# Masks of the ranked layer on GpSimd, written as complements, and their exponents split evenly between VectorE and ScalarE

## The chip, the cores and the metric

One core of one Trainium2 chip runs the whole program. The metric is the device time of an execution in microseconds (us), from runs repeated three times; lower is better. A profiled execution of the same kernel gives the trace from which all durations below are read. The engines are TensorE (PE, with its weight loads shown as PEld), VectorE (DVE), ScalarE (ACT), GpSimd (POOL) and SyncE (SP), which here only issues transfers.

## The reference

A graph of N = 3327 nodes with 64 features each passes through four layers, every one of the form x = x + layer(relu(layernorm(x))) with the same dense adjacency matrix `adj` (3327 x 3327 floats, few of them non-zero):

- layer 0: two gated cells; each multiplies `adj` by the features and feeds a GRU
- layer 1, "ranked": only the last 100 neighbours of a row count, and each weighs half of the one after it
- layer 2: three products with `adj * adj` (element by element), each followed by a linear map
- layer 3: two products with `adj`, each followed by a linear map and tanh

So `adj` is read for eight products, called steps k = 0 to 7 in the kernel. Step 2 is the ranked one:

```python
mask = (adj != 0).astype(support.dtype)
rank = jnp.cumsum(mask, axis=1)
deg = rank[:, -1:]
k = jnp.minimum(deg, float(MAX_NEIGH))
pos = rank - (deg - k)
w = mask * jnp.where(pos > 0, DECAY ** (k - pos), 0.0)
out = w @ support + bias
```

The weight of a neighbour is a power of two that depends only on how many neighbours come after it in its row.

## The kernel before, in words

The nodes are padded to 26 blocks of 128 (two halves of 13 blocks). The adjacency matrix lies transposed in memory, so a tile is 128 source nodes (tile number q, 26 of them) by the target nodes of one group. There are two groups of target columns, `GROUPS`: group 0 holds chunks 0 and 1 (3 + 3 blocks of 128), group 1 holds chunks 2 and 3 (3 + 4 blocks). Each group is taken from both halves of the nodes, so a tile has two halves (s = 0, 1) of 768 columns in group 0 and of 896 in group 1. `Tile.load` (L405) issues one transfer per tile on SP's queue into one of 20 slots (`slots`, shown as `adj` in the profile); the slot must have been given up by its last user, `Tile.used`.

The steps are interleaved in pairs per group so that one load serves two steps: `joint(0, 1)` is steps 1 and 2 of group 0, `joint(1, 2)` is steps 2 and 3 of group 1. The function `run` walks a fixed list of units (step, chunk, tile), and looks ahead: up to 44 units for loads, 24 for masks, 3 for the expansion. All engines work through their instructions in the order in which this walk emits them; nothing is reordered at run time. Side work of each chunk (GRU, layer norm and so on, `after_0` to `after_7`) is a generator that is advanced by an amount of PE time (`spend`).

For the ranked step a tile goes through these stages:

1. `make_mask` (L466) writes the mask, 1.0 where `adj` is not zero, as bfloat16 for 127 of the 128 rows, in two "pieces" (one per half). Between the two, L471 has POOL issue a small transfer that puts the counts of all later blocks (`totals`) into row 127 of the mask. After the second piece the raw tile has been `used` once, which, in group 0 at step 2, gives its slot up. Masks lie in slots too, two to a slot; `Mask` takes one and `free` returns it after the tile's last expansion.
2. `expand` (L510 to L523) multiplies the mask by a triangular matrix `tri` on PE (L307). `tri` has 2^14 on its diagonal and -2^7 below it, and row 127 takes the counts with -2^7, so each sum is the bit pattern of the weight's exponent, short of the constant `BITS`. Adding `BITS` and clamping at zero, written as a 16-bit integer and read as bfloat16, is the weight. This last operation is L521 on DVE (a constant added, then the maximum with zero) or L523 on ACT (Relu with `bitsb` as bias). A rule with several cases picks DVE or ACT for half s = 1; half s = 0 is always on ACT.
3. `propagate` (L607) multiplies the weights by the features, held as three bfloat16 terms (`both`), which `in_three` splits off.

POOL also does one operation of each layer norm (L845, a power of -1/2), issues the transfers that collect the last row of each block (`lasty`, L928), and clears the scratch of `last_sources` (L564), whose two small transfers (L568) stand in SP's queue among the loads. The counts come from an earlier pass (`count`, L542) over masks of all 128 rows, which L466 also writes, on DVE; there are 104 pieces of this kind and 104 of the ranked kind.

Of the kernel before, what the change touches and what calls it, by code (L numbers as in the profile page):

```python
# [9 lines left out]
F32 = mybir.dt.float32  # L10
BF16 = mybir.dt.bfloat16
I16 = mybir.dt.int16
AF = mybir.ActivationFunctionType
ALU = mybir.AluOpType
# [30 lines left out]
N, D = 3327, 64  # L45
P = 128
NB = 13
# [8 lines left out]
GROUPS = [(0, 1), (2, 3)]  # L56
GWM = 7 * P
EPS = 1e-5
TWO7 = float(2 ** 7)
TWO27 = float(2 ** 27)  # L60
CAP = 100.0
BITS = (CAP - 128.0) * TWO7
# [8 lines left out]
PLAIN, RANKED, SQUARED = range(3)  # L71
# [12 lines left out]
def chunk_of(b):  # L84
    return next(c for c, (b0, b1) in enumerate(CH[:NC]) if b0 <= b < b1)
# [6 lines left out]
def upper(n):  # L92
    return slice(n * D, (n + 1) * D)
# [3 lines left out]
def kernel(  # L97
# [9 lines left out]
    nc = tc.nc  # L107

    const = ctx.enter_context(tc.tile_pool(name="const", bufs=1))
# [8 lines left out]
    for g0, g1 in (CH[0], (CH[0][1], NB)):  # L118
# [15 lines left out]
    make_identity(nc, ident)  # L134
    tri = const.tile([P, P], BF16, name="tri")
    behind = const.tile([P, NQ - 1 + D], BF16, name="behind")
    bitsb = const.tile([P, 1], F32, name="bitsb")
    totals = [const.tile([P, sum(CH[c][1] - CH[c][0] for c in g) * P], BF16, name=f"totals{i}")
              for i, g in enumerate(GROUPS)]
    lastw = [const.tile([P, sum(CH[c][1] - CH[c][0] for c in g) * P], I16, name=f"lastw{i}")  # L140
             for i, g in enumerate(GROUPS)]
# [7 lines left out]
                            compare_op=ALU.is_gt, fill=0.0, base=2 - P, channel_multiplier=1)  # L149

    def load_cell(cell):
        nc.sync.dma_start(out=stage[upper(0), :7 * D].rearrange("p (w f) -> p w f", f=D),
                          in_=weights[:, (W1, W2)[cell]:(W1, W2)[cell] + 7])
        if cell == 0:
            nc.sync.dma_start(out=stage[upper(0), 7 * D:], in_=bias_cols)
# [82 lines left out]
    def more_constants():  # L238
        nc.gpsimd.memset(stage, 0.0)
        nc.gpsimd.memset(cells, 0.0)  # L240
        for c in range(NC):
            for h in range(2):
                nc.gpsimd.memset(both[c][upper(h), h], 0.0)
        nc.gpsimd.memset(bd, 0.0)
        yield 5.0
        load_cell(0)
        yield 20.0
        unfold_cell(0)
        yield 1.0

        full = work.tile([P, P], BF16, name="t2")
        nc.gpsimd.memset(full, -TWO7)
        nc.gpsimd.affine_select(out=tri, in_=full, pattern=[[-1, P]], compare_op=ALU.is_gt, fill=0.0,
                                base=0, channel_multiplier=1)
        nc.gpsimd.affine_select(out=tri, in_=tri, pattern=[[-1, P]], compare_op=ALU.not_equal, fill=TWO7 * TWO7,
                                base=0, channel_multiplier=1)
        nc.gpsimd.memset(tri[:, P - 1:P], 0.0)
        nc.gpsimd.memset(bitsb, BITS)
        nc.gpsimd.memset(lasty, 0.0)
        wide = work.tile([P, P], F32, name="t2")  # L260
        nc.gpsimd.memset(wide, 0.0)

        for i, (bi, bh) in enumerate(((BI1, BH1), (BI2, BH2))):
            nc.vector.tensor_add(bsum[:, i], bcol[:, bi:bi + 2], bcol[:, bh:bh + 2])

        nc.vector.tensor_scalar(wide[0:D], wide[0:D], bcol[0:D, BL1:BL1 + 1], None, op0=ALU.add)
        yield 3.0
        i, ps = take()
        mm(ps[:, :D], wide, ident[:, :D])
        nc.vector.tensor_copy(brow[:, 3], ps[:, :D])  # L270
        give(i)
        yield 1.0
        yield from fold_cell(0)
        for c in range(NC):
            yield 1.0
            ahead_of_cell(c)
        yield 50.0
        load_cell(1)
        yield 20.0
        unfold_cell(1)  # L280
        yield from fold_cell(1)
        yield 30.0
        for h in range(2):
            nc.sync.dma_start(out=bd[upper(h), :, upper(h)], in_=weights[:, WL1:WL3])
            for i in range(2):
                nc.sync.dma_start(out=w3[upper(h), :, i], in_=weights[:, WL3 + (h + i) % 2:NW:2])
        yield 5.0
        nc.sync.dma_start(
            out=brow[:, 0:3],
            in_=bass.AP(tensor=bias_rows.tensor, offset=bias_rows.offset, ap=[[0, P], [D, 3], [1, D]]),  # L290
        )
        yield 22.0
        yield from fold_hops()
# [5 lines left out]
    def width(c):  # L299
        return blocks(c) * P  # L300

    def mm(out, lhsT, rhs, start=True, stop=True):


        for h in range(2):
            hs = slice(h * D, (h + 1) * D)
            nc.tensor.matmul(out[hs], lhsT[:, hs], rhs, start=start, stop=stop)  # L307
# [21 lines left out]
    def give(i):  # L329
        released[i] = max(released) + 1  # L330
        (idle_sums if i < 4 else idle_temps).append(i)
# [34 lines left out]
    def finish(c):  # L366
        while c in tasks:
            advance(c)
# [16 lines left out]
    sums = {}  # L385
# [70 lines left out]
    pieces = deque()  # L456

    relief = {"squares": False, "pieces": False}

    def make_mask(t, kind):  # L460

        t.mask = Mask(t.w)
        rows = P - 1 if kind == RANKED else P

        def piece(half):
            nc.vector.tensor_scalar(t.mask.view[:rows, half], t.view()[:rows, half], 0.0, None, op0=ALU.not_equal)  # L466
            if half == 0 and kind == RANKED:

                for ch in GROUPS[t.g]:
                    finish(("count", ch))  # L470
                nc.gpsimd.dma_start(out=t.mask.view[P - 1:P], in_=totals[t.g][t.q:t.q + D + 1:D, :])  # L471
            if half == 1:
                t.used()

        pieces.extend([(t, 0, piece), (t, 1, piece)])
# [8 lines left out]
    def expand(k, c, t):  # L484

        if k == COUNT:
            return None
        w = width(c)
        if t is SPECIAL:
            g = c // 2  # L490
            w0 = (CH[c][0] - CH[GROUPS[g][0]][0]) * P
            finish(NC + 1 + g)
            return lastw[g][:, w0:w0 + w].bitcast(BF16)
        if KIND[k] == PLAIN or (KIND[k] == SQUARED and t.in_place):
            return t.view(c)
        if KIND[k] == SQUARED:
            room = Mask(t.w)
            wide = room.view.rearrange("p s w -> p (s w)").bitcast(F32)[:, :2 * w].rearrange("p (s w) -> p s w", s=2)
            square(wide, t.view(c), t.q + c)
            squared[k, c, t] = room  # L500
            return wide
        wide = work.tile([P, 2, CWM], I16, name="e", bufs=4)[:, :, :w]

        mask_pieces(t=t)
        for s in range(2):
            i, ps = take()
            mm(ps[:, :w], tri, t.mask.view[:, s, t.cols(c)])  # L510
            own = chunk_of(t.q % NB) in GROUPS[t.g]
            busy = any((k - 1, ch) in sums for ch in GROUPS[t.g])
            if t.g == 1 and not own and not relief["squares"]:

                on_vector = s and c == GROUPS[1][1]
            elif relief["pieces"]:
                on_vector = s and (t.q + c) % 4
            else:
                on_vector = s and (own if t.g == 0 and (own or busy) else c == GROUPS[t.g][1] or t.g == 1 and not own)
            if on_vector:  # L520
                nc.vector.tensor_scalar(wide[:, s], ps[:, :w], BITS, 0.0, op0=ALU.add, op1=ALU.max)  # L521
            else:
                nc.scalar.activation(wide[:, s], ps[:, :w], AF.Relu, bias=bitsb)  # L523
            give(i)
        spend(STREAM_US * w / CWM * 0.5)
        if c == GROUPS[t.g][1]:
            t.mask.free()
        return wide.bitcast(BF16)
# [29 lines left out]
    def last_sources(g):  # L558

        w = sum(width(c) for c in GROUPS[g])  # L560
        w0 = CH[GROUPS[g][0]][0] * P
        room = Mask(w)
        v = room.view.rearrange("p s w -> p (s w)").bitcast(F32)
        nc.gpsimd.memset(v, 0.0)  # L564
        yield 4.0
        rows = adjT.rearrange("(q p) (s n) -> q p s n", p=P, s=2)
        for s in range(2):
            nc.sync.dma_start(out=v[s * D:s * D + NQ], in_=rows[:, P - 1, s, w0:w0 + w])  # L568
        yield 12.0
        nc.vector.tensor_scalar(v, v, 0.0, 129.0 * TWO7, op0=ALU.not_equal, op1=ALU.mult)  # L570
        for c in GROUPS[g]:
            finish(("count", c))
        yield 1.0
        nc.vector.scalar_tensor_tensor(v, totals[g], -TWO7, v, op0=ALU.mult, op1=ALU.add)
        yield 1.5
        nc.scalar.activation(lastw[g], v, AF.Relu, bias=bitsb)
        room.free()

    def propagate(k, c, t, rhs, first, last):
# [506 lines left out]
```

## Time and profile before

| what | value |
|---|---|
| median of the runs | 706.3 us (705.96 to 706.94) |
| the profiled execution, first to last instruction (its span) | 703.7 us |
| PE, weight loads, DVE, ACT, POOL busy | 679.8, 372.9, 350.1, 271.8, 80.0 us |
| L466, all mask pieces, on DVE | 208 pieces, 114.0 us |
| of these the ranked ones: 127x768 and 127x896 | 52 at 567 ns and 52 at 619 ns |
| L521 on DVE | 63 in all |
| L523 on ACT | 145 in all |
| L471 on POOL | 52, mean 607 ns |
| SP's loads of tiles | 130 of 768 KB, 104 of 896 KB |

The profiled execution's own time is its span, which lies 2.6 us under the median of the runs; the difference is what surrounds the program, and is taken as constant. Times inside the trace count from the start of the span. Busy time is the sum of an engine's instructions, and the number after a group of instructions is the mean duration of one. "Idle before" a group names what released its engine. In the timeline a row can hold several instructions (the number after x).

### The profile page before, as it was taken

The page shows a single profiled execution, that of the slowest core. Times are in us where ns is not written, and L with a number is a line of the kernel's source. Part 1 is how long each engine was busy: PE and PEld are TensorE (multiplying, and loading weights), DVE is VectorE, ACT ScalarE, POOL GpSimd, SP SyncE. Part 2 cuts the span into 40 slices and gives each one's busy share as a digit, 9 for nine tenths or more (in the row PEclk, how much of TensorE's full clock was granted, in tenths as well). Part 3 has the DMA queues.
Part 4 walks back from the last instruction along what each step waited for, and adds up shares of the span by engine and source line. Part 5 has one row for each costly group of instructions (what it writes and reads, how often), then busy time and mean ns, then how long its engine had stood idle before and what let it go on. Part 6 is the DMA issues. An engine that isn't in the chain of part 4 may idle for free.

```text
span 703.7 us, 12628 instructions
## 1 busy us (share of the span) xinstructions
PE 679.8 (97%) x5100; PEld 372.9 (53%) x5100; DVE 350.1 (50%) x746; ACT 271.8 (39%) x422; POOL 80.0 (11%) x114
## 2 busy tenths in 40 slices
PE   1999999999999999999999999999999999999997
PEld 1454666643556787677444444333344444344586
DVE  7556835643997889847523105425271565005101
ACT  1014100122146888888998206832166600000101
POOL 4300000002284233111100000000000000000000
PEclk9999999999999999999999999999999999999999
DMA  9999996089686952683799649973998399927991
GB/s 344 401 385 404 406 405 241 2 314 398 209 279 253 371 177 76 246 297 96 265 390 343 245 151 409 405 276 100 398 366 271 107 391 406 406 81 276 402 403 45
DMA packets 68549, 201.31 MB, mean 286 GB/s; under 512 B 7228, under 2 KB 8228, under 8 KB 68492
## 3 DMA queue, kind: packets, MB, share of 16 engines
q1 hardware_dynamic: 65596, 199.46, 75.9%
q8 instruction: 40, 0.66, 0.4%
q10 hardware_dynamic: 720, 0.85, 0.3%
q0 software_dynamic: 2176, 0.20, 0.2%
q14 instruction: 17, 0.14, 0.1%
HBM read 199.45 MB, written 0.85 MB: 285 GB/s over the span
## 4 chain that ended last, share of the span: by engine, by line
PE 91%; DVE 7%; issue 0%; ACT 0%; DMA 0%; POOL 0%; ACTq 0%; DVEq 0%; POOLq 0%
PE sum L607 77%; PE temp L307 5%; PE temp L542 2%; PE temp L876 2%; PE sum L307 1%; DVE adj L466 1%; PE temp L774 1%; PE sum L876 1%; DVE e L521 1%; DVE st L842 1%; DVE adj L901 1%; DVE t L836 1%; DVE y L841 0%; DVE st L834 0%; DMA xs<-in_x 0%
## 5 line engine op out<-in xcount | busy, mean ns | idle before, releaser
L607 PE MATMUL sum<-adj,y 128*64 128x384 f32 (+3 forms) x3016 | 534.5, 502 | 0.7 <-DVE y L849 0.6
L607 PEld LDWEIGHTS sum<-adj,y 128*64 128x64 f32 x3016 | 243.5, 137 | 237.3 <-issue 212.4
L440 ACT ACTIVATE adj<-adj 128x768 f32<-128x768 f32 (+1 forms) x176 | 144.2, 893 | 45.8 <-PE sum L607 21.9
L466 DVE TENSOR_SCALAR adj<-adj 128x768 bf16<-128x768 f32 (+3 forms) x208 | 114.0, 597 | 39.8 <-PE temp L542 31.8
L824 ACT COPY both<-sum 64x384 f32<-64x384 f32 (+3 forms) x17 | 8.1, 478 | 192.6 <-PE sum L607 191.4
L607 PE MATMUL sum<-e,both 128*64 128x384 bf16 (+1 forms) x624 | 78.5, 339 | 0.5 <-DVE e L521 0.5
L523 ACT ACTIVATE e<-temp,bitsb 128x384 int16<-128x384 f32 (+1 forms) x117 | 66.0, 605 | 15.1 <-PE temp L307 9.9
L825 DVE COPY both<-sum 64x384 f32<-64x384 f32 (+3 forms) x17 | 9.6, 569 | 110.5 <-ACT both L824 110.5
L307 PE MATMUL temp<-adj,tri 128*64 128x384 bf16 (+1 forms) x332 | 56.8, 341 | 0.5 <-DVE e L521 0.2
L442 DVE TENSOR_TENSOR adj<-adj 128x768 f32<-128x768 f32 (+1 forms) x32 | 30.6, 1005 | 52.1 <-DMA adj<-in_adjT 33.4
L845 POOL TENSOR_TENSOR st<-st,mhalf 128x6 f32<-128x6 f32 (+1 forms) x16 | 24.0, 1498 | 283.2 <-DVE st L843 279.5
L607 PEld LDWEIGHTS <-both 128*64 128x64 bf16 x624 | 46.6, 110 | 15.5 <-issue 2.2
L307 PEld LDWEIGHTS <-tri 128*64 128x64 bf16 x416 | 33.5, 110 | 15.3 <-issue 7.1
L521 DVE TENSOR_SCALAR e<-temp 128x384 int16<-128x384 f32 (+1 forms) x49 | 30.1, 617 | 21.1 <-ACT e L523 10.5
L471 POOL DMA_DIRECT2D adj<-totals x52 | 31.5, 607 | 51.2 <-PE temp L307 40.9
L803 DVE STREAM_TRANSPOSE both<-y 32x96 f32<-32x96 f32 (+1 forms) x128 | 35.6, 278 | 2.9
L542 PE MATMUL temp<-adj,behind 128*64 128x384 bf16 x208 | 30.3, 339 | 0.9 <-DVE adj L466 0.7
L819 DVE STREAM_TRANSPOSE y<-t 32x96 f32<-32x96 f32 (+1 forms) x64 | 17.8, 278 | 24.9 <-ACT t L810 24.0
L542 PEld LDWEIGHTS <-behind 128*64 128x64 bf16 x208 | 17.0, 110 | 17.6 <-issue 15.9
L755 DVE COPY t<-sum 128x384 f32<-128x384 f32 x6 | 3.3, 555 | 35.3 <-PE sum L607 35.3
L564 POOL MEMSET adj<- 128x768 f32 (+1 forms) x2 | 1.9, 950 | 145.3 <-PE sum L607 145.3
L523 ACT ACTIVATE e<-sum,bitsb 128x384 int16<-128x384 f32 (+1 forms) x28 | 16.6, 598 | 2.5 <-PE sum L307 2.1
(132 smaller groups left out, 327.8 us busy)
## 6 DMA issues: line engine op xcount, KB each, us to landing
adj<-in_adjT SPq DMA_DIRECT2D x130, 768.0 KB, 8.5
adj<-in_adjT SPq DMA_DIRECT2D x104, 896.0 KB, 12.3
xs<-in_x SPq DMA_DIRECT2D x1, 640.0 KB
adj<-totals POOLq DMA_DIRECT2D x26, 3.0 KB, 5.1
adj<-totals POOLq DMA_DIRECT2D x26, 3.5 KB, 3.0
out<-xs ACTq DMA_DIRECT2D x2, 192.0 KB
out<-xs ACTq DMA_DIRECT2D x1, 256.0 KB
stage<-in_weights SPq DMA_DIRECT2D x2, 112.0 KB, 13.1
```

Source lines behind the costliest of these rows:

```text
L307: nc.tensor.matmul(out[hs], lhsT[:, hs], rhs, start=start, stop=stop)
L440: nc.scalar.activation(sq, v, AF.Square)
L442: nc.vector.tensor_tensor(sq, v, v, ALU.mult)
L466: nc.vector.tensor_scalar(t.mask.view[:rows, half], t.view()[:rows, half], 0.0, None, op0=ALU.not_equal)
L471: nc.gpsimd.dma_start(out=t.mask.view[P - 1:P], in_=totals[t.g][t.q:t.q + D + 1:D, :])
L521: nc.vector.tensor_scalar(wide[:, s], ps[:, :w], BITS, 0.0, op0=ALU.add, op1=ALU.max)
L523: nc.scalar.activation(wide[:, s], ps[:, :w], AF.Relu, bias=bitsb)
L542: nc.tensor.matmul(counts[c][1][s * D:(s + 1) * D, :w], behind[:, NQ - 1 - t.q:NQ - 1 - t.q + D], t.mask.view[:, s, t.cols(c)], start=firs ...
L607: nc.tensor.matmul(acc[h][1][h * D:(h + 1) * D, :w], yq[h], rhs[h], start=first and n == 0, stop=last and n == len(terms) - 1)
L803: nc.vector.transpose(to[at:at + 32, :, q], h[q * 32:(q + 1) * 32, :, s, f * 32:(f + 1) * 32])
L845: nc.gpsimd.tensor_tensor(st[:, 3, :n], st[:, 2, :n], mhalf[:, :n], ALU.pow)
L876: nc.tensor.matmul(ps[upper(1 - s), :w], cells[:, cell, s, g, :], both[c][:, s], start=True, stop=True)
```

## The change

The ranked masks are written by GpSimd and not by VectorE, and as complements: 1.0 where `adj` is zero. The triangular matrix changes its sign in rows 0 to 126, while row 127, which meets the counts, keeps -2^7 through one more `affine_select`. What the complement adds to each sum depends only on the row of the result, so a bias per partition replaces the constant: four small PE instructions multiply `tri` by a column of ones, and a small DVE instruction turns the result into `bitsb[:, 0:1]`; `bitsb[:, 1:2]` holds the old constant for `last_sources`. The masks of the counting pass stay on DVE, unchanged. In `expand` the rule with cases goes: half 0 is always on ScalarE, half 1 always on VectorE.

```diff
-    bitsb = const.tile([P, 1], F32, name="bitsb")
+    bitsb = const.tile([P, 2], F32, name="bitsb")
...
-        nc.gpsimd.memset(full, -TWO7)
+        nc.gpsimd.memset(full, TWO7)
...
-        nc.gpsimd.affine_select(out=tri, in_=tri, pattern=[[-1, P]], compare_op=ALU.not_equal, fill=TWO7 * TWO7,
+        nc.gpsimd.affine_select(out=tri, in_=tri, pattern=[[-1, P]], compare_op=ALU.not_equal, fill=-TWO7 * TWO7,
                                 base=0, channel_multiplier=1)
+        nc.gpsimd.affine_select(out=tri, in_=tri, pattern=[[0, P]], compare_op=ALU.is_gt, fill=-TWO7,
+                                base=P - 1, channel_multiplier=-1)
         nc.gpsimd.memset(tri[:, P - 1:P], 0.0)
-        nc.gpsimd.memset(bitsb, BITS)
+        nc.gpsimd.memset(bitsb[:, 1:2], BITS)
...
         mm(ps[:, :D], wide, ident[:, :D])
+        for h in range(2):
+            nc.tensor.matmul(ps[upper(h), D:D + 2], tri[:P - 1, upper(h)], behind[:P - 1, 0:2], start=True, stop=True)
         nc.vector.tensor_copy(brow[:, 3], ps[:, :D])
+        nc.vector.tensor_scalar(bitsb[:, 0:1], ps[:, D:D + 1], -1.0, BITS, op0=ALU.mult, op1=ALU.add)
...
-            nc.vector.tensor_scalar(t.mask.view[:rows, half], t.view()[:rows, half], 0.0, None, op0=ALU.not_equal)
+            if kind == RANKED:
+                nc.gpsimd.tensor_scalar(t.mask.view[:rows, half], t.view()[:rows, half], 0.0, None, op0=ALU.is_equal)
+            else:
+                nc.vector.tensor_scalar(t.mask.view[:rows, half], t.view()[:rows, half], 0.0, None, op0=ALU.not_equal)
...
-            own = chunk_of(t.q % NB) in GROUPS[t.g]
-            busy = any((k - 1, ch) in sums for ch in GROUPS[t.g])
-            if t.g == 1 and not own and not relief["squares"]:
-
-                on_vector = s and c == GROUPS[1][1]
-            elif relief["pieces"]:
-                on_vector = s and (t.q + c) % 4
+            on_vector = s == 1
+            if on_vector:
+                nc.vector.tensor_scalar(wide[:, s], ps[:, :w], bitsb[:, 0:1], 0.0, op0=ALU.add, op1=ALU.max)
             else:
-                on_vector = s and (own if t.g == 0 and (own or busy) else c == GROUPS[t.g][1] or t.g == 1 and not own)
-            if on_vector:
-                nc.vector.tensor_scalar(wide[:, s], ps[:, :w], BITS, 0.0, op0=ALU.add, op1=ALU.max)
-            else:
-                nc.scalar.activation(wide[:, s], ps[:, :w], AF.Relu, bias=bitsb)
+                nc.scalar.activation(wide[:, s], ps[:, :w], AF.Relu, bias=bitsb[:, 0:1])
...
-        nc.scalar.activation(lastw[g], v, AF.Relu, bias=bitsb)
+        nc.scalar.activation(lastw[g], v, AF.Relu, bias=bitsb[:, 1:2])
```

## The prediction

> **What bounds the kernel now.** I read the page's busy times and groups first:
>
> ```profile
> PE 679.8 (97%) x5100; PEld 372.9 (53%) x5100; DVE 350.1 (50%) x746; ACT 271.8 (39%) x422; POOL 80.0 (11%) x114
> L466 DVE TENSOR_SCALAR adj<-adj 128x768 bf16<-128x768 f32 (+3 forms) x208 | 114.0, 597 | 39.8 <-PE temp L542 31.8
> L523 ACT ACTIVATE e<-temp,bitsb 128x384 int16<-128x384 f32 (+1 forms) x117 | 66.0, 605 | 15.1 <-PE temp L307 9.9
> ```
>
> PE sets the end. Its matmuls also run at full cadence: 8 float matmuls of 384 columns in 1.29 us recur all over the chain. Pricing every matmul at its own cadence (float 384: 0.161 us, bfloat16 0.080 us), I find about 0.1 us lost per 10 us nearly everywhere, but 10.7 us between 170 and 350 us, the ranked stretch. At most about 9 us are therefore to be won. The windows of that stretch show who is short there:
>
> ```profile
> 200.00:205.00 5.00, 5.00 (x38) 2.42 (x36) 5.00 (x10) 2.57 (x5) 4.07 (x7) 1.00 1.01 368
> 205.00:210.00 5.00, 5.00 (x48) 3.16 (x46) 5.00 (x11) 3.48 (x8) 4.73 (x3) 1.00 0.81 273
> 210.00:215.00 5.00, 5.00 (x35) 2.87 (x33) 4.55 (x10) 2.07 (x4) 5.00 (x5) 1.00 0.01 1
> 240.00:260.00 20.00, 19.93 (x239) 16.46 (x236) 15.91 (x32) 17.45 (x35) 7.23 (x13) 1.00 0.76 253
> ```
>
> Columns: length, then PE, PEld, DVE, ACT, POOL busy, clock, DMA share. DVE is full until 215, ACT nearly so at 250. Between 210 and 215 no load moves. SP's timeline tells why pieces matter beyond DVE:
>
> ```profile
> 178.40 10.23 SPq L405 DMA_DIRECT2D adj<-in_adjT  x4
> 192.96 1.26 SPq L405 DMA_DIRECT2D adj<-in_adjT  x2
> 196.50 9.93 SPq L405 DMA_DIRECT2D adj<-in_adjT  x4
> 215.36 0.73 SPq L568 DMA_DIRECT2D adj<-in_adjT  x2
> ```
>
> These ten loads are the last step-1 tiles of group 0. Nearly all of them wait for a mask piece to give up the slot. The last is issued at 205.9, right after the second piece of ranked tile 16 (ended 205.85), its bytes end near 210, and PE reads it from about 210.3 on: less than 1 us of slack. The pieces of tile 16 set PE's pace here.
>
> How POOL and DVE meet (DVE's and POOL's timelines), and what POOL's streaming costs (groups by shape):
>
> ```profile
> 206.34 6.18 DVE L466 TENSOR_SCALAR adj<-adj 127x768 bf16<-127x768 f32 x13
> 206.72 7.47 POOL L928 DMA_DIRECT2D lasty<-both  x4 [0.27 <-DVE both L921]
> L148 POOL TENSOR_SCALAR_AFFINE_SELECT behind<-behind 128x1 bf16<-128x1 bf16 x1 | 0.2, 187 | 0.1
> L253 POOL TENSOR_SCALAR_AFFINE_SELECT tri<-t 128x128 bf16<-128x128 bf16 x1 | 0.3, 292 | 0.1
> L240 POOL MEMSET cells<- 128x1024 f32 x1 | 0.9, 947 | 0.0
> ```
>
> While DVE ran 13 pieces back to back, the first of four POOL transfers took 5.90 us; the other twelve of its kind have a median of 0.51. Last, POOL late in the ranked step:
>
> ```profile
> 321.31 0.54 POOL L471 DMA_DIRECT2D adj<-totals  x1 [1.35 <-PE temp L307]
> 323.21 1.65 POOL L471 DMA_DIRECT2D adj<-totals  x3 [1.35 <-PE temp L307]
> ```
>
> There POOL waits for mask buffers that PE gives back every 1.9 us, and the last pieces end at 327.3, as PE wants them.
>
> **The skill.** "GPSIMD Engine Reference", Performance versus the Vector engine, gives 1.03 cycles per element for short loop bodies, about 1.8 for a tight loop otherwise, at 1.2 GHz; its engine table calls one-input operations roughly line-rate. The trace agrees with the lower figure for memset (947 ns at 1024) and affine_select ((292 - 187)/127 = 0.83 ns per element, one cycle); the operation itself isn't in it. "SBUF — State Buffer", Who interferes with whom: a DVE operation in a two-port mode, or with two SBUF inputs, excludes a POOL operation that reads SBUF for its whole length, and the reverse; the 5.90 us agree. "TensorE: Matmul & The Clock Gate", The HAM clock gate: after some 3.4 us idle PE drops to half clock. The start agrees: the first 12 of L791 took 1.55 us, twelve later ones 0.66.
>
> **The change, part by part.**
>
> Removed from DVE: 104 ranked pieces, 52 x 567 + 52 x 619 ns = 61.7 us of latency, about 57 of busy time. The split of exponents goes from 63 on DVE and 145 on ACT to 104 and 104: 41 x 0.6 = 25 us move to DVE. Net DVE -32, ACT -25 us. PE waits there for other reasons too (the GRU's and layer norm's chains), so I credit 3 of the 9 us; bounds 0 and 9.
>
> The setup adds one affine_select (0.29 us) on POOL, four PE matmuls of two columns and a small DVE operation (0.14). Done near 30 us, needed at 203; their cover is that gap. PE is full then, so its four cost 0.2 us, or 0.5 if uncovered.
>
> Added to POOL: 104 compares. Price, an estimate from affine_select's 187 ns plus 0.83 per further element: 0.82 us (768) and 0.93 (896). Bounds: below, 0.70 and 0.80, if the starting part overlaps the operation before, as in back-to-back use it may; above, at 1.8 cycles (1.5 ns per element), 1.34 and 1.53. I take 0.82 and 0.93.
>
> First stall, tile 16. In the changed instruction order POOL has, up to its second piece: the memset until 171.0; 34 pieces, 27.9; 17 row transfers of 0.54, 9.2; two powers of L845 at about 1.6, 3.2; four transfers of L928 at 0.51, 2.0. That is 213.3. DVE's two-input operations between 171 and 214 sum to 9.9 us; excluded both ways, some of it delays POOL. I take half, 5 (bounds 0 and 10): 218.3. Before it was 205.85; less 0.8 of slack: 11.6 us of PE stall. The bounds give 3 (0.70, no locks) to 17. The loads behind tiles 12 and 13 come late too, by 2 and 4 us, inside the same stall. Behind the waiting load on SP stand L568 and all loads of group 1; they move by as much as PE, so nothing adds.
>
> Next in line on POOL: the power for chunk 0's layer norm, which stands behind all 26 tiles. 171.0 + 42.6 + 14.0 + 3.2 + 4.1 + 1.0 (second memset) + 8 of locks = 244. Its input came at 235.2 and comes 11.6 later, at 247, so it isn't held. With 1.34 us per piece it would be near 271.
>
> Second stall, the last six tiles of group 1. Mask buffers come free at 317.1, 319.0, 320.9, 322.8. A tile now costs POOL 2 x 0.93 + 0.54 = 2.40 us, where PE takes a tile per 0.92. Run through: tile 20 starts at 317.6, 21 at 320.0, 22 at 322.4, and so on to 25 at 329.6; its row transfer is issued at 330.5 and lands some 2.4 later (as the one of 323.2 did for 325.6), at 332.9. PE wanted it at 327.3: 5.6 us. With 0.80 it is 4, with 1.53 POOL is late throughout.
>
> Half clock after stalls of that length: 2 us (0 to 4).
>
> Sum: 0.2 + 11.6 + 5.6 + 2 - 3 = +16.4. Against the execution's 703.7 that is 720.1; the same difference on the median of 706.3 gives 722.7, say 722.
>
> **Rivals.**
>
> Slow compares. POOL's arithmetic may run at 1.8 cycles; for it speaks that the power takes 1411 ns on six elements, so stock operations on POOL can be slow; against it, affine_select's one cycle. Then group 0's work ends at 171 + 69.7 + 22 + 8 = 271; group 1 starts some 14 later, behind L928, and needs 26 x 3.60 + 3 = 97, to 382 plus 2 of landing, where PE wanted 327.3. POOL is the bound: +57, 763.
>
> Locks to the full, 10 us and not 5, with DVE's chains waiting for POOL in turn: 17 + 6 + 4 - 1 = +26, 732. For it speaks the 5.90 us; against it, L466 itself, the cause there, is gone from these windows.
>
> Faster. Mechanism: the relief of DVE and ACT. It decides once tile 16 is done by 206.7, which needs pieces of about 0.62 us and no locks, and the sweep costs less than the relief. At 0.65, first stall 1, second 3, relief 8: -4, 702. Against it: 768 elements at one per cycle are already 0.64 us.
>
> Hidden anyway. Stall and relief cancel within a microsecond: 706.3; needs 0.70 and nearly the whole relief.
>
> **How the numbers follow.** The three runs spread over 1.0 us; about 0.2%, 1.4 us, is what a measurement of this kernel can tell from no change. Chances: the forecast, 712 to 728, 0.50; full locks or a price between the two, to 745, 0.18; slow compares 0.21; faster 0.07; no change 0.04. The range leaves out the upper part of the slow case and most of the fast one: 707 to 764. Faster 0.07, same 0.04, slower 0.89.
>
> **What would show it.** L472's compares on POOL near 0.82 and 0.93 us start to start. PE idle near 211 us for about 12 us, released by a load whose slot a POOL piece gave up. PE idle again in the last six ranked tiles of group 1, on POOL's piece or row transfer. DVE and ACT below 80% from 200 to 340. The stretch after 350 as long as before. It is wrong if the compares take over 1.2 us (then POOL is full from 171 to 380), if group 0's loads are still early, or if the lost cadence of 170 to 350 comes back whole.

## The result and the profile after

The changed kernel takes 841.6 us (841.2 to 842.3) where the kernel before takes 706.6 us (706.0 to 707.9, the three runs above and one more): a ratio of 1.191, with a 95% interval from 1.189 to 1.193. The forecast said 722 us with a range from 707 to 764. Its sign was right; its size was not, and the time lies far outside its range. Of the rivals, "slow compares" named the right mechanism, but its price was too low as well.

The page of the changed kernel, its busy times, two rows of the 40 slices, and the group that the change adds:

```profile
span 840.6 us, 12750 instructions
PE 712.2 (85%) x5102; PEld 377.0 (45%) x5102; DVE 346.8 (41%) x684; ACT 256.0 (30%) x381; POOL 308.2 (37%) x219
POOL 5100000089999979999999100000000001000000
PEclk9999999999565989879955899999999999999999
L472 POOL TENSOR_SCALAR adj<-adj 127x768 bf16<-127x768 f32 (+1 forms) x104 | 238.2, 2304 | 2.0
```

POOL's 37% over the whole span hides what its slices show: it is all but full from slice 9 to slice 22, and nearly idle elsewhere. Its busy time rose by 228 us: the new compares (L472) add 238.2, and its other instructions fell by 10. The same groups by shape (columns after the bar: busy us, mean ns of one, idle before):

```profile
L472 POOL TENSOR_SCALAR adj<-adj 127x896 bf16<-127x896 f32 x52 | 126.9, 2453 | 1.0
L472 POOL TENSOR_SCALAR adj<-adj 127x768 bf16<-127x768 f32 x52 | 111.4, 2155 | 1.0
```

A compare takes 2.155 and 2.453 us where the forecast put 0.82 and 0.93. Between the two shapes lie 298 ns for 128 columns.

The windows of the ranked stretch (length, then PE, PEld, DVE, ACT, POOL busy, clock, DMA share, GB/s), the same stretches as the prediction shows of before, and one later:

```profile
200.00:205.00 5.00, 5.00 (x34) 2.05 (x30) 0.00 (x0) 0.00 (x0) 4.97 (x4) 1.00 0.58 173
205.00:210.00 5.00, 2.38 (x18) 0.95 (x16) 3.05 (x5) 0.51 (x1) 4.96 (x5) 1.00 0.67 194
210.00:215.00 5.00, 2.41 (x8) 0.76 (x9) 3.23 (x3) 0.51 (x1) 4.97 (x4) 0.61 0.01 1
240.00:260.00 20.00, 3.72 (x21) 1.09 (x15) 0.00 (x0) 0.00 (x0) 19.86 (x16) 0.63 0.21 75
440.00:460.00 20.00, 7.88 (x38) 3.10 (x37) 2.47 (x4) 2.21 (x4) 19.85 (x13) 0.50 0.00 1
```

Before, PE worked 19.93 of the 20 us from 240 to 260; now it works 3.72, DVE and ACT not at all, and POOL 19.86. From 440 to 460 PE has work for 7.88 us, at half its clock, and no load moves. POOL is the bound of this stretch.

SP's own timeline shows the loads that the prediction followed (start, length, then line and what is moved):

```profile
205.55 11.87 SPq L410 DMA_DIRECT2D adj<-in_adjT  x2
226.47 33.14 SPq L410 DMA_DIRECT2D adj<-in_adjT  x4
271.52 0.73 SPq L568 DMA_DIRECT2D adj<-in_adjT  x2
286.10 38.16 SPq L410 DMA_DIRECT2D adj<-in_adjT  x15
```

The last step-1 loads of group 0 are issued between 226 and 259, where before they were out at 205.9, and L568, the step behind them on SP, comes at 271.5 and not at 215.4. The last pieces of group 1 on POOL close the chain:

```profile
448.95 4.87 POOL L472 TENSOR_SCALAR adj<-adj 127x896 bf16<-127x896 f32 x2
453.77 0.58 POOL L479 DMA_DIRECT2D adj<-totals  x1
454.39 4.88 POOL L472 TENSOR_SCALAR adj<-adj 127x896 bf16<-127x896 f32 x2
459.21 0.58 POOL L479 DMA_DIRECT2D adj<-totals  x1
459.83 2.46 POOL L472 TENSOR_SCALAR adj<-adj 127x896 bf16<-127x896 f32 x1
```

No row has idle time before it: a tile costs POOL 5.44 us from start to start, and PE gets one tile per 5.44 us. The last piece ends at 462.3. Before, it ended at 327.4 us. This shift, 134.9 us, is the whole result but for 2 us: the span grew by 136.9.

### The profile page after: what moved, and what is told of

The parts are those of the page before. It is cut to its first block, busy times and chain, and to the rows that moved or that the text cites. A ratio compares the mean times of both kernels' runs of the same rounds, so it can differ in the third digit from the quotient of the medians.

```text
span 840.6 us, 12750 instructions
## 1 busy us (share of the span) xinstructions
PE 712.2 (85%) x5102; PEld 377.0 (45%) x5102; DVE 346.8 (41%) x684; ACT 256.0 (30%) x381; POOL 308.2 (37%) x219
## 4 chain that ended last, share of the span: by engine, by line
PE 45%; POOL 6%; issue 1%; DVE 1%; DMA 1%; ACT 0%; ACTq 0%; POOLq 0%; DVEq 0%
PE sum L607 42%; POOL adj L472 5%; PE temp L312 1%; PE temp L774 1%; DMA adj<-totals 1%; POOL adj L479 0%; POOL st L845 0%; DVE xs L1019 0%; ACT t L1016 0%; DVE both L825 0%; ACT both L824 0%; DVE e L521 0%; ACTq L1021 0%; PE sum L312 0%; DVE t L836 0%
## 5 line engine op out<-in xcount | busy, mean ns | idle before, releaser
L472 POOL TENSOR_SCALAR adj<-adj 127x768 bf16<-127x768 f32 (+1 forms) x104 | 238.2, 2304 | 2.0
L607 PE MATMUL sum<-e,both 128*64 128x384 bf16 (+1 forms) x624 | 87.8, 387 | 30.5 <-ACT e L523 20.3
L845 POOL TENSOR_TENSOR st<-st,mhalf 128x6 f32<-128x6 f32 (+1 forms) x16 | 22.8, 1429 | 241.0 <-DVE st L843 241.0
L312 PE MATMUL temp<-adj,tri 128*64 128x384 bf16 (+1 forms) x332 | 61.9, 398 | 45.6 <-DMA adj<-totals 21.1
L521 DVE TENSOR_SCALAR e<-temp,bitsb 128x384 int16<-128x384 f32 (+1 forms) x82 | 52.8, 651 | 86.5 <-PE temp L312 71.8
L523 ACT ACTIVATE e<-temp,bitsb 128x384 int16<-128x384 f32 (+1 forms) x84 | 50.7, 607 | 78.0 <-PE temp L312 63.3
L474 DVE TENSOR_SCALAR adj<-adj 128x768 bf16<-128x768 f32 (+1 forms) x104 | 57.0, 601 | 40.0 <-PE temp L542 32.1
L607 PEld LDWEIGHTS <-both 128*64 128x64 bf16 x624 | 48.8, 124 | 52.9 <-issue 40.3
L819 DVE STREAM_TRANSPOSE y<-t 32x96 f32<-32x96 f32 (+1 forms) x64 | 17.8, 278 | 24.4 <-ACT t L810 23.5
L312 PE MATMUL sum<-adj,tri 128*64 128x384 bf16 (+1 forms) x84 | 16.6, 368 | 5.4 <-DVE e L521 4.8
## 6 DMA issues: line engine op xcount, KB each, us to landing
adj<-in_adjT SPq DMA_DIRECT2D x104, 896.0 KB, 13.5
```

Source lines behind the costliest of these rows:

```text
L472: nc.gpsimd.tensor_scalar(t.mask.view[:rows, half], t.view()[:rows, half], 0.0, None, op0=ALU.is_equal)
L521: nc.vector.tensor_scalar(wide[:, s], ps[:, :w], bitsb[:, 0:1], 0.0, op0=ALU.add, op1=ALU.max)
L607: nc.tensor.matmul(acc[h][1][h * D:(h + 1) * D, :w], yq[h], rhs[h], start=first and n == 0, stop=last and n == len(terms) - 1)
L845: nc.gpsimd.tensor_tensor(st[:, 3, :n], st[:, 2, :n], mhalf[:, :n], ALU.pow)
```

## The experiments

Theory: POOL's row of compares is the bound of the ranked stretch, and the forecast failed at the price of a compare, not at its reasoning. Rivals: the even split of the exponents, or the bias column, costs much by itself; the order on POOL's queue (powers and transfers behind pieces) costs much whatever the price; the loss comes from one group only.

### What a POOL operation costs by itself

The kernel before, with extra POOL operations on a spare slot in a late step, where POOL is idle. Three of each. The whole took 705.5 us in its single run.

```diff
+        forms = [(d16, src, ALU.is_equal), (d16, src, ALU.is_gt), (d32, src, ALU.is_equal),
+                 (d16[:, :512], src16, ALU.is_equal), (d16[:, :512], src[:, :512], ALU.is_equal),
+                 (d16[:, :128], src[:, :128], ALU.is_equal), (d16, src, ALU.mult), (d32, src, ALU.mult)]
+        for to, at, op in forms:
+            for _ in range(3):
+                nc.gpsimd.tensor_scalar(to, at, 2.0, None, op0=op)
...
+                nc.gpsimd.tensor_copy(to, src)
...
+            nc.gpsimd.affine_select(out=d32, in_=src, pattern=[[-1, 768]], compare_op=ALU.is_gt, fill=0.0,
+                                    base=0, channel_multiplier=1)
```

> The kernel before with 13 forms of POOL operations added on a spare slot, three of each, near 590 us where VectorE is nearly idle (the kernel loses a buffer, so its own time may be some us longer). A: comparing is slow, then is_equal and is_gt take 2.1 us at 768 and mult and copy about 0.8 to 1.0. B: the conversion from float32 to bfloat16 is slow, then all float32 to float32 forms take about 0.9 and all mixed ones 2.1. C: every tensor_scalar on POOL runs at about 3 cycles per element, whatever the operation and type, and only copy, memset and affine_select are at one. The width tells the slope: 128, 512 and 768.

POOL's groups by shape in that kernel (L722 holds the two compares and the multiplication of f32 to bf16 in its first row, compare and multiplication of f32 to f32 in its second; L725 is the copy):

```profile
L722 POOL TENSOR_SCALAR adj<-adj 127x768 bf16<-127x768 f32 x9 | 19.2, 2135 | 0.8
L722 POOL TENSOR_SCALAR adj<-adj 127x768 f32<-127x768 f32 x6 | 12.8, 2129 | 0.5
L732 POOL TENSOR_SCALAR adj<-adj 64x768 bf16<-64x768 f32 x3 | 6.4, 2129 | 0.3
L722 POOL TENSOR_SCALAR adj<-adj 127x512 bf16<-127x512 f32 x3 | 4.5, 1487 | 0.2
L722 POOL TENSOR_SCALAR adj<-adj 127x512 bf16<-127x512 bf16 x3 | 4.5, 1487 | 0.2
L725 POOL CAST adj<-adj 127x768 bf16<-127x768 f32 x3 | 2.5, 828 | 0.2
L727 POOL TENSOR_SCALAR_AFFINE_SELECT adj<-adj 127x768 f32<-127x768 f32 x3 | 2.5, 828 | 0.2
L730 POOL MEMSET adj<- 127x768 f32 x3 | 2.2, 738 | 0.2
L722 POOL TENSOR_SCALAR adj<-adj 127x128 bf16<-127x128 f32 x3 | 1.6, 527 | 0.2
```

Neither the comparison nor the types nor the number of partitions matter: every form of tensor-with-constant operation tried takes 2.13 us over 768 columns. From 128 to 768 columns it is (2135 - 527)/640 = 2.51 ns per element, with some 205 ns fixed. Copy and affine_select take 828 ns, which is the forecast's 0.82 within a hundredth: its estimate was right for affine_select and was carried to an operation that costs 2.6 times as much. Of the three answers the last one, C, holds: this whole form of operation is slow. Why it is, no run here shows.

### The forecast at its own price

The copy costs what the forecast believed of the compare. With it in the compare's place, the forecast's arithmetic can be tried at its own price:

```diff
-                nc.gpsimd.tensor_scalar(t.mask.view[:rows, half], t.view()[:rows, half], 0.0, None, op0=ALU.is_equal)
+                nc.gpsimd.tensor_copy(t.mask.view[:rows, half], t.view()[:rows, half])
```

> The changed kernel with a plain copy from f32 to bf16 on GpSimd in the place of each compare, over the same columns; what the ranked step counts is then not the ranks, and that part of the computation is left out. The copy took 828 ns over 768 columns where it was measured alone, which is the price that the forecast gave the compare. Theory (only the price was wrong, the forecast's sum is right at its own price): 715 to 730 us, PE idle for about 12 us near 211 us. Rival (the order on GpSimd's queue, with powers and row transfers behind the pieces, costs much even at that price): 735 to 765 us. Rival (at that price all is hidden): 700 to 710 us.

Measured: 728.6 us, ratio 1.033 (1.030 to 1.035), which is 22.0 us over before, where the forecast's sum was +16.4. POOL's groups by shape, then PE's timeline at the first stall, then SP's:

```profile
L472 POOL CAST adj<-adj 127x896 bf16<-127x896 f32 x52 | 48.1, 946 | 13.5 <-issue 8.7 <-PE temp L312 3.8 <-POOL adj L472 1.0
L472 POOL CAST adj<-adj 127x768 bf16<-127x768 f32 x52 | 44.3, 881 | 0.0
```

```profile
213.32 2.23 PE L607 MATMUL sum<-adj,y 128*64 128x384 f32 x12
222.15 2.19 PE L607 MATMUL sum<-adj,y 128*64 128x384 f32 x6 [6.59 <-DMA adj<-in_adjT]
```

```profile
199.41 18.36 SPq L410 DMA_DIRECT2D adj<-in_adjT  x4
224.16 0.72 SPq L568 DMA_DIRECT2D adj<-in_adjT  x2
```

This is the forecast's first stall, in its place and for its reason: the second piece of tile 16 ends at 217.2 (forecast 218.3), the last load of group 0 is issued 0.03 us after it, and PE waits 6.6 us for it. POOL has idle time in group 1 again (13.5 us in the first row), so it is no bound here.

The same with the old rule for the exponents separates the split:

> The copies on GpSimd as above, and the rule of before for the exponents; the ranks are left out as above. Theory (with the masks off VectorE the even split is hidden): within 3 us of the kernel with copies and the even split. Rival (the even split costs its 19 us here too): 15 to 20 us faster than that.

Measured: 725.0 us (1.027; 1.024 to 1.029), 3.6 us less than with the even split: close to the theory, a little beyond its 3 us. The even split is not quite hidden. It seems to act between 240 and 260 us, where VectorE works 19.49 of 20 us with the even split and 18.03 with the old rule, and PE 14.98 and 18.12.

### A price in between

Each copy is followed by a second one over half of its columns:

```diff
-                nc.gpsimd.tensor_scalar(t.mask.view[:rows, half], t.view()[:rows, half], 0.0, None, op0=ALU.is_equal)
+                nc.gpsimd.tensor_copy(t.mask.view[:rows, half], t.view()[:rows, half])
+                nc.gpsimd.tensor_copy(t.mask.view[:rows, half, :t.w // 2], t.view()[:rows, half, :t.w // 2])
```

> The copies on GpSimd again, and after each one a second copy over the first half of its columns: about 1.27 us a piece in group 0 and 1.42 in group 1, near the upper price that the forecast's rival named. The ranks are left out, as above. Theory (GpSimd becomes the bound and the rival's rule holds: group 0 ends at 171 + 52 x 1.27 + 24 = 261, group 1 starts 12 later and takes 26 x 3.4 + 3 = 91, plus 2 to land, 366 where 327.3 was wanted): +39 us, 740 to 755 us. Rival (the time grows evenly with the piece's length between the kernel with single copies and the one with compares): 765 to 775 us.

Measured: 763.7 us (1.082; 1.080 to 1.085), inside neither range. The length that the expectation put in was short. In POOL's groups by shape the two copies of a pair add to more than that:

```profile
L472 POOL CAST adj<-adj 127x896 bf16<-127x896 f32 x52 | 48.7, 937 | 0.0
L472 POOL CAST adj<-adj 127x768 bf16<-127x768 f32 x52 | 44.7, 860 | 0.0
L473 POOL CAST adj<-adj 127x384 bf16<-127x384 f32 x52 | 31.0, 596 | 3.3
L473 POOL CAST adj<-adj 127x448 bf16<-127x448 f32 x52 | 30.6, 589 | 3.3
```

Where nothing else stands between them, a pair starts 1.35 us after the pair before it in group 0 and 1.51 in group 1. By chance that is almost the 1.34 and 1.53 of the forecast's rival, which was worked out on record before any run: group 0 done at 271, the last piece at 382, and 763 us in all. The last pairs end at 269.7 and 384.9, and the time is 763.7. The rule of that rival is therefore right to about 3 us in each of its steps. The even growth that the expectation's rival assumed, taken at the true 1.35 us and with 0.77 and 2.12 us from start to start for the copies and the compares, would give 728.6 + 113 x 0.58/1.35 = 777, which is 13 too high.

### Which group, and do they add

GpSimd writes the ranked masks of group 0 alone, or of group 1 alone; VectorE the others, as complements. For group 1 the condition reads `t.g == 1`.

```diff
-                nc.gpsimd.tensor_scalar(t.mask.view[:rows, half], t.view()[:rows, half], 0.0, None, op0=ALU.is_equal)
+                engine = nc.gpsimd if t.g == 0 else nc.vector
+                engine.tensor_scalar(t.mask.view[:rows, half], t.view()[:rows, half], 0.0, None, op0=ALU.is_equal)
```

> POOL writes the masks of group 0 only, VectorE those of group 1. POOL's queue for group 0 ended 69 us later than before (317.8 instead of 249.1, when group 1's masks can begin), so 706.6 + 66 = 773 us, 765 to 780. Rival: the two groups' delays hide behind one another, then this alone is above 800.

> POOL writes the masks of group 1 only. They start at 249 as before and need 26 tiles x (2 x 2.45 + 0.6) + 3 = 146 us, to 395 and 2 more for the row to land, where PE wanted the last at 327.3: +70, 776 us, 768 to 782. The two groups alone then add up to the whole +135. Rival: above 800, or under 750 if buffers and not POOL's rate set the pace.

Measured: 782.6 us (1.108; 1.105 to 1.110) and 785.1 us (1.111; 1.108 to 1.114). Both are some 3 us over the top of what was expected (2.6 and 3.1), for the same reason as the next run's miss: each still has one group whose masks and half of the exponents are both on VectorE. So the two excesses over before, 76 and 78 us, do not add up to the whole +135, as had been expected: they give 154. Against the kernel with all ranked masks on VectorE and the even split (725.8 us, the next run) they do: 56.9 and 59.3 make 116.2, and both groups together cost 115.8.

### The split, the bias column and the turned sign

The masks go back to VectorE as complements, once with the even split, once with the rule of before; and the changed kernel gets the rule of before.

```diff
-                nc.gpsimd.tensor_scalar(t.mask.view[:rows, half], t.view()[:rows, half], 0.0, None, op0=ALU.is_equal)
+                nc.vector.tensor_scalar(t.mask.view[:rows, half], t.view()[:rows, half], 0.0, None, op0=ALU.is_equal)
```

```diff
-            on_vector = s == 1
+            own = chunk_of(t.q % NB) in GROUPS[t.g]
+            busy = any((k - 1, ch) in sums for ch in GROUPS[t.g])
+            if t.g == 1 and not own and not relief["squares"]:
+                on_vector = s and c == GROUPS[1][1]
+            elif relief["pieces"]:
+                on_vector = s and (t.q + c) % 4
+            else:
+                on_vector = s and (own if t.g == 0 and (own or busy) else c == GROUPS[t.g][1] or t.g == 1 and not own)
```

First diff alone:

> The changed kernel with its ranked masks written by VectorE again (still as complements, with the bias per partition and the even split of exponents). If the compares on POOL are the whole cause, the time returns to 704 to 712 us; VectorE then has 104 pieces and 104 exponents, about 31 us more than before in the ranked stretch, so up to 5 us over 706.6. Rival: the split or the bias column costs by itself (each of the 104 exponents on VectorE took 0.06 us more in the changed kernel's trace); then it stays above 720.

Measured: 725.8 us (1.027; 1.025 to 1.029), and not the 704 to 712 of the expectation: its rival holds. Both diffs:

> The masks back on VectorE as complements, the bias column kept, and the rule of before for the exponents. Theory (the 19 us of the kernel with vector masks come from the even split, which gives VectorE some 40 exponents more in the stretch where it is already over 80% busy): 706 to 711 us. Rival (they come from the bias column, 59 ns more on each exponent of VectorE, and from the turned sign): 718 to 727 us.

Measured: 708.0 us (1.002; 1.001 to 1.003). So the bias column and the turned sign, with their setup, cost 1.5 us together, and the even split costs 17.8 when VectorE also writes the masks. The windows from 205 to 215 us of the kernel with masks on VectorE and the even split, and PE's timeline there, show how it begins:

```profile
205.00:210.00 5.00, 1.35 (x12) 0.53 (x8) 5.00 (x10) 0.79 (x2) 4.80 (x10) 0.96 0.69 224
210.00:215.00 5.00, 4.54 (x22) 2.05 (x24) 5.00 (x11) 0.58 (x2) 3.49 (x6) 0.50 0.17 44
208.57 0.65 PE L607 MATMUL sum<-e,both 128*64 128x384 bf16 x5 [3.20 <-DVE e L521]
```

VectorE is full, and exponents of the first ranked tiles stand in its queue behind mask pieces: its first one runs at 207.9, where in the kernel before ScalarE writes all of them until 220.3. PE waits for the exponent, not for the mask. From 165 to 365 us its waits for VectorE's exponents sum to 12.3 us, where before they were 2.1 and with the old rule 2.6; for the masks it waits 2.4.

Second diff alone, on the changed kernel:

> The changed kernel with the rule of before for the half whose exponents VectorE writes; GpSimd's compares and the bias column stay. Theory (GpSimd's row of compares alone sets the stretch from 171 to 463 us): within 4 us of the changed kernel, 838 to 845 us, and the last compare of group 1 still ends near 462 us. Rival (the even split adds its own 19 us here too, as it does with the masks on VectorE): 818 to 828 us.

Measured: 842.9 us (1.194; 1.191 to 1.196). The interval of its ratio overlaps that of the changed kernel (1.189 to 1.193). Where POOL is the bound, the split is worth nothing, and the last compare ends at 463.0, as in the changed kernel within a microsecond. The split costs nothing with compares on POOL, 3.6 us with copies there and 17.8 with masks on VectorE: one edit, priced by who is full beside it.

### The powers behind the compares

In the changed kernel PE's first long stall is not the one that was forecast. PE's, then DVE's timeline:

```profile
210.64 2.41 PE L607 MATMUL sum<-adj,y 128*64 128x384 f32 x8 [2.91 <-DMA adj<-in_adjT]
233.39 0.48 PE L607 MATMUL sum<-e,both 128*64 128x384 bf16 x1 [20.34 <-ACT e L523]
247.35 1.55 PE L607 MATMUL sum<-adj,y 128*64 128x384 f32 x4 [4.06 <-DMA adj<-in_adjT]
```

```profile
228.11 1.00 DVE L848 TENSOR_SCALAR st<-st 128x8 f32<-128x8 f32 x1 [14.88 <-POOL st L845]
229.14 0.69 DVE L849 SCALAR_TENSOR_TENSOR y<-t,st 128x512 f32<-128x512 f32 x1
232.89 1.41 DVE L921 TENSOR_TENSOR both<-y,both 128x512 bf16<-128x512 f32 x1 [0.69 <-ACT both L919]
```

The power of the second layer norm of group 0 (L845) stands behind the pieces on POOL and runs at 226.4. DVE, which issues in order, waits 14.9 us at L848, and behind it wait the rows (`both`) and the exponents that PE needs; ScalarE's own rows (L919) wait for DVE, and ScalarE's exponents stand behind them. This route isn't in the prediction, which counted the powers in POOL's time but followed, as a path, only that of chunk 0 at the end of the group. Is it on the path that sets the end?

```diff
-        nc.gpsimd.tensor_tensor(st[:, 3, :n], st[:, 2, :n], mhalf[:, :n], ALU.pow)
+        nc.vector.tensor_tensor(st[:, 3, :n], st[:, 2, :n], mhalf[:, :n], ALU.mult)
```

> The changed kernel with the power of the layer norm left out: a product of the same size on VectorE stands in its place, so the norm isn't computed, and no power waits behind GpSimd's compares. Theory (GpSimd's queue sets the stretch, and PE's first stall of 20 us, 213 to 233, lies inside it): only GpSimd's own time is saved, 8.4 us of powers between 171 and 463 and up to 5 of its idle time at 308 to 315: 826 to 836 us. Rival (the powers' place behind the compares is itself on the path, and the first stall's 20 us come back whole): 815 to 822 us.

Measured: 836.2 us (1.185; 1.183 to 1.187), 0.2 us over the upper edge of the theory and far from the rival. PE's timeline in that kernel:

```profile
212.22 2.83 PE L607 MATMUL sum<-adj,y 128*64 128x384 f32 x8 [2.84 <-DMA adj<-in_adjT]
221.98 2.68 PE L607 MATMUL sum<-adj,y 128*64 128x384 f32 x8 [5.09 <-DMA adj<-in_adjT]
231.25 1.55 PE L607 MATMUL sum<-adj,y 128*64 128x384 f32 x4 [5.09 <-DMA adj<-in_adjT]
240.74 1.54 PE L607 MATMUL sum<-adj,y 128*64 128x384 f32 x4 [7.94 <-DMA adj<-in_adjT]
246.00 1.55 PE L607 MATMUL sum<-adj,y 128*64 128x384 f32 x4 [3.72 <-DMA adj<-in_adjT]
```

The single wait of 20.3 us is gone, but PE's idle time from 204 to 248 us falls only from 29.8 us in sum to 24.7, and all of it is now waits on loads, each issued some 0.03 us after the end of the POOL piece that gives up its slot. The forecast's mechanism stood behind the other one. The last compare ends 5.0 us earlier (457.3), about what POOL saves inside the two groups; the gap between them stays (11.7 us, and 12.1 with the powers).

### Is there anything to win

The forecast credited 3 us, at most 9, to the relief of VectorE. The kernel before, with 8 or all 16 of the first second pieces of group 0 written on ScalarE, where it is nearly idle (the diff is that for 8; for 16 the last condition is left out):

```diff
+        turn = made[0]
+        made[0] += kind == RANKED
...
-            nc.vector.tensor_scalar(t.mask.view[:rows, half], t.view()[:rows, half], 0.0, None, op0=ALU.not_equal)
+            if kind == RANKED and t.g == 0 and half == 1 and turn < 16 and turn % 2 == 0:
+                nc.scalar.activation(t.mask.view[:rows, half], t.view()[:rows, half], AF.Tanh, scale=256.0)
+            else:
+                nc.vector.tensor_scalar(t.mask.view[:rows, half], t.view()[:rows, half], 0.0, None, op0=ALU.not_equal)
```

> The kernel before, with the second piece of every other one of the first 16 ranked tiles of group 0 written by ScalarE as tanh(256 x), which is 1 for every entry of 0.05 or more: 8 pieces of 0.57 us leave VectorE where it is full, for 8 of about 0.84 us on ScalarE, which works 2.2 of 20 us there. Theory (VectorE's queue costs PE 2 to 4 us between 200 and 240): 703 to 706 us. Rival (those losses are chains that VectorE's load doesn't set): 706 to 708 us.

> The same for all of the first 16 second pieces: 16 pieces leave VectorE. Theory (as above): 702 to 705 us. Rival: 706 to 708 us, or above 708 if ScalarE, which issues in order, now holds its squares and exponents behind pieces that wait for loads.

Measured: 705.4 and 705.3 us, both 0.9987 of before (0.9979 to 0.9996, and 0.9979 to 0.9995). Both intervals lie just under 1. If this is a gain, it is 1.2 and 1.4 us, below the 0.2% that the prediction called measurable, and twice the pieces don't double it. The windows of before (first two lines) and of the kernel with 16 pieces on ScalarE:

```profile
200.00:220.00 20.00, 20.00 (x151) 11.44 (x148) 17.28 (x33) 11.47 (x22) 18.07 (x20) 1.00 0.60 205
220.00:240.00 20.00, 18.55 (x235) 13.68 (x235) 17.72 (x39) 14.24 (x29) 2.13 (x2) 1.00 1.03 406
200.00:220.00 20.00, 20.00 (x154) 11.07 (x150) 11.18 (x23) 9.29 (x19) 11.83 (x16) 1.00 0.79 273
220.00:240.00 20.00, 18.56 (x234) 13.60 (x231) 17.60 (x37) 14.73 (x30) 1.65 (x2) 1.00 0.96 342
```

VectorE fell from 17.28 to 11.18 us in the first stretch, and PE's 18.56 of 20 us in the second is what it was (18.55). So VectorE's load in the stretch of group 0's masks doesn't set what PE loses from 220 to 240; the chains there remain as the likely cause, not tested further. The masks of group 1 stayed on VectorE in both kernels, so what their relief is worth stays open. The median of no version here lies more than 0.2% under that of the kernel before.

### One table for all of them

The end of the last ranked piece, on whichever engine, against the span of each profiled execution. Before it is 327.4 and 703.7 us.

| Kernel | group 0's pieces end | group 1's, from - to | last piece later by | span longer by |
|---|---|---|---|---|
| before | 221.3 | 252.0 - 327.4 | 0 | 0 |
| masks on VectorE, even split | 229.2 | 263.9 - 347.7 | 20.3 | 20.0 |
| copies on POOL | 239.1 | 266.9 - 349.0 | 21.6 | 21.7 |
| copies, a half twice | 269.7 | 288.1 - 384.9 | 57.4 | 58.4 |
| compares for group 0 | 306.5 | 320.4 - 404.2 | 76.8 | 76.6 |
| compares for group 1 | 228.1 | 260.0 - 404.9 | 77.5 | 79.1 |
| changed kernel, no powers | 304.0 | 315.7 - 457.3 | 129.9 | 131.3 |
| changed kernel | 305.7 | 317.8 - 462.3 | 134.9 | 136.9 |

The last two columns agree within 2 us in every row: after the last piece nothing is won back, and little is lost. The groups also add, in the time that each takes. Compares make group 0 end at 305.7 or 306.5, whatever group 1 does, and make group 1 take 144.5 or 144.9 us, whatever group 0 did. On VectorE with the even split group 1 takes 83.8 us in both kernels that have it so.

## Why the prediction was wrong

**The price of a compare: the step that failed.** "Price, an estimate from affine_select's 187 ns plus 0.83 per further element: 0.82 us (768) and 0.93 (896)." The runs have 2.155 and 2.453. The bounds failed with it: the upper one, 1.34 and 1.53, was worked out from the 1.8 cycles of the Trainium skill's "GPSIMD Engine Reference", Performance versus the Vector engine. That page calls 1.8 the best case of a tight loop, and the prediction used it as an upper bound. At the page's 1.2 GHz the 2.51 ns measured here are an estimated 3.0 cycles per element; "roughly line-rate", which its table in Engine selection says of one-input operations, holds for copy in these runs (828 ns) and not for the compare. The trace of before had no tensor-with-constant operation on POOL at all. The row next to it in kind, the power on six elements at 1411 ns, was named in the prediction and not used as a warning for the bound.

**Which side POOL falls on.** The prediction put the point from which POOL is the bound at 1.2 us a compare, and that its rule is right above that point shows in the kernel with pairs of copies (1.35 and 1.51). The point itself was not tried: with single copies (0.88 and 0.95) POOL is no bound. Fed with the measured price the rule gives: group 0 to 171 + 52 x 2.155 + 22 + 8 = 313, group 1 from 327, 26 x (2 x 2.453 + 0.54) + 3 = 145, the last piece at 472; measured 305.7, 317.8 and 462.3. It is some 10 us high in all, of which 7 lie in group 0, mostly in the 8 put in for locks. So with the right price the prediction would have said about 853 us for 841.6.

**First stall, 11.6 us.** At the forecast's price it is 6.6 us of idle PE at the place and for the reason given. It is shorter in the main because PE came later: it had already lost 3.3 us at 185 us (see the locks). In the changed kernel tile 16's second piece ends at 259.0. PE had stopped long before, by the route through the power and DVE's queue, which the prediction hadn't listed.

**Locks.** Five to eight us of POOL's time were put in for DVE's two-input operations. POOL's compares lost almost nothing: 2155 ns in the mean against 2135 alone, 1 us over the 52; the copies lost 2.8 us (881 against 828). The cost went the other way. The Trainium skill's "SBUF — State Buffer", Who interferes with whom, says that the exclusion holds in both directions, and DVE paid: L901 over 384 columns took 675 ns in the mean for 553 before. In the kernel with copies PE stood 3.3 us at 185 us for such a chain, in which L835, with one input, took 1.45 us and not 0.17, and the two-input L836 1.67 and not 0.56; the same wait was 0.22 us before. The prediction's sum had no term for that.

**Second stall, 5.6 us.** With copies PE waits 3.0 us in sum in front of the last tiles, for row transfers, as forecast; a tile cost POOL 2.29 us there, forecast 2.40. In the changed kernel POOL is late throughout: PE waits 11 times for a row transfer (21.1 us) and 10 times for a piece (8.7 us).

**Relief, -3 us, bounds 0 and 9.** Some 1.4 us for the 16 of group 0's 52 pieces that were moved, and 1.2 for 8; for the rest, and for group 1, it was not measured. The even split, which was only counted as busy time moved, costs 3.6 us with copies on POOL.

**Half clock, 2 us.** PE's busy time grew by 32 us in the changed kernel, with a mean granted clock of 0.924 (0.50 from 440 to 460), in agreement with the half clock after idle time of the Trainium skill's "TensorE: Matmul & The Clock Gate", The HAM clock gate. Nearly all of it lies in POOL's shadow, since the span grew by only 2 us more than the end of the last piece. With copies the clock is 0.94 from 200 to 220 and 0.80 from 220 to 240, and 1.00 before: an estimate of at most 0.06 x 20 + 0.20 x 20 = 5 us, so the 2 may have been short.

**The setup, 0.2 us.** It was counted as hidden, and the complement with its bias costs 1.5 us in the kernel that keeps all else. The part left out is the bias read as a column by each exponent on VectorE: 613 ns and not 554 over 384 columns. Which of the two makes the 1.5 us was not separated.

At its own price the forecast's sum was 16.4, the run 22.0. The forecast had too much for the first stall (6.6 measured) and the second (3.0), and nothing for DVE's own waits (3.3 less 0.2) and the split (3.6); with the 1.5 of the setup these make 17.8, and what is left is within the estimate for the half clock. These parts were not all measured apart from one another. With these errors alone the time stays inside the range (728.6 us). The price alone took it out.

## What to carry to other kernels

An operation that has no row in the trace has no upper bound either: a neighbour's rate and a "best case" bound it only from below, so leave the slow side of the range wide, or time three of the operation in an idle stretch first. Then ask at which price the engine becomes the bound of its stretch (work queued on it over time available), because past that point every further nanosecond is multiplied by the number of pieces, and little else in the change matters: here the split was worth nothing and the powers 5.3 us. An edit to the split between two engines has no price of its own; the same edit was worth 0, 3.6 and 17.8 us here.

## What the runs showed of the hardware

- On POOL a tensor-with-constant operation (compare or multiplication, f32 or bf16, 64 or 127 partitions) took 2.51 ns per element and about 205 ns fixed: 527 ns at 128 columns, 1487 at 512, 2135 at 768. Copy with conversion and affine_select took 828 ns at 768, memset 738.
- Two copies on POOL of which the second reads what the first read and writes over a part of its output started 0.90 us apart, against 0.77 for copies that follow each other without such an overlap.
- On DVE the exponent with a column for its bias took 613 ns over 384 columns and 747 over 512, against 554 and 688 with a constant: 59 ns more at both lengths.
- POOL in back-to-back use delayed DVE's operations on SBUF far more than these delayed POOL: in the changed kernel L901 took 675 ns for 553 and the small one-input L835 398 for 172, while POOL's compares took 2155 for 2135. DVE's exponents, which read the results of matmuls and not SBUF, took the same time with compares on POOL as with masks on VectorE (614 and 612 ns).
